# Attention scores of a non-local layer: contraction over 96 rows in one piece, or over three parts of 32 rows on four row groups

## The chip, the cores and the metric

The kernel runs on one core of one Trainium2 chip. The core has five engines, each with its own queue of instructions: TensorE (PE, matrix products; its weight loads are listed separately as PEld), VectorE (DVE), ScalarE (ACT), GpSimd (POOL) and SyncE (SP, which here only issues transfers). The metric is the device time of the whole kernel in microseconds (us); before the change it is 6844.52 us, the median of three runs (6835.98 to 6856.77). All data are 32-bit floats, and every product `nc.tensor.matmul` appears in the trace as two weight loads and two matmuls.

## The reference

A batch of 4 images of 192 channels and 64x64 pixels passes through four layers: a deformable convolution with channel attention and an MLP (layer 0), a non-local block (layer 1), overlapping-window attention with a gated MLP (layer 2), and a per-image depthwise convolution (layer 3). The change concerns layer 1 alone:

```python
g_x     = conv1x1(x, g_w, g_b)          # 96 channels, N = 4096 pixels
theta_x = conv1x1(x, theta_w, theta_b)  # the queries, 96 channels
phi_x   = conv1x1(x, phi_w, phi_b)      # the keys, 96 channels
f1 = einsum('bon,bom->bnm', theta_x, phi_x)   # 4096 x 4096 scores an image
y  = einsum('bnm,bom->bon', softmax(f1, axis=-1), g_x)
return conv1x1(y, W_w, W_b) + x
```

## The kernel before

The images go one after another through the layers. Each image `b` has a **keys stage** (`keys`, from L859), then **layer 1** proper (`layer1`, from L880), then layer 2's windows (L1112 and around it are its scores), and the MLPs with layer 3. Work of the next image is woven in: for images 0, 1 and 2, the gather of the next image's layer 0 (`gather`, L566 to L596, four interpolating operations on ACT and DVE for each of 297 gathers, and products `h`, L590) runs beside layer 1, some 2.5 gathers a step; for images 1 and 2 the offsets of the next image (`offsets`, L431 to L490: layer norm, a table written to DRAM, a convolution `po`) run beside the keys stage. Image 3 has nothing beside it.

**Keys stage.** The image `x` lies in DRAM (`x_drams`), as two halves of 96 channels. For each of 8 chunks of 512 pixels, x is loaded (L865), two products accumulate `phi` (L868) into one bank of PSUM, and ACT copies it with its bias to `ph`, 96 rows by 4096 keys (L869). Eight products make `g` transposed (L873), and DVE copies it to `gx` (L876).

**Layer 1.** The 4096 queries are cut into 16 tiles of 256 (`NQ`, `QN`), the keys into 8 groups of 4 x 128 (`NG`, `G`): 128 steps an image. For each query tile, `load` fetches x (L909), projects it to 96 query channels (L912), and ACT adds the bias (L914). For each step, `score` makes four products of 96 rows, 128 keys, 256 queries (L920) into a PSUM tile `p` of two banks, of which the pool has two; ACT copies it to one of the slots in SBUF (L922), and DVE keeps the running maximum (L925, L927). After a tile's eighth step `negated_max` folds it, transposes it on PE (L936), negates it (L938), spreads it over 128 rows (L941, L944) and copies it (L946).

The scores run ahead of their use: `ahead` is the number of slots, 10 beside a gather and 16 for image 3. The main loop then adds the negated maximum (L983, DVE), takes the exponential (L984, ACT) and multiplies with `gx` into `py` (L986, PE, four products); after each step it issues the scores of the step `ahead` later into the slot just read. `finish` divides by the sum (the gx column of ones), applies `W` (L960), adds the kept x (L961), and stores the result.

**Order.** A planner lays out each engine's queue when the program is built, from the order of the text, estimated durations, and the buffers' becoming free; the hardware runs each queue in that order. `in_turn` pins a constant's load behind what stands before it on SP. PSUM has eight banks: four for the scores, two for `a` and `y`, and two for the gather's `h0`, `h1`.

The central lines of `score`:

```python
for t in range(G):
    nc.tensor.matmul(p[:, t, :], lhsT=ph[:, bass.ts(G * g + t, 128)], rhs=ths[i], start=True, stop=True)
nc.scalar.copy(slot(i, g), p)
```

Of the kernel before, what the change touches and what calls it, by code (L numbers as in the profile page):

```python
# [13 lines left out]
ALU = mybir.AluOpType  # L14
# [33 lines left out]


QN, G, EXTRA = 256, 4, 2  # L50
NQ, NG = HW // QN, HW // 128 // G


# [26 lines left out]
def conv_seq_kernel(ctx: ExitStack, tc: tile.TileContext, a, out: bass.AP):  # L80
    nc = tc.nc

    def pool_of(**kw):

        return tc.tile_pool(**({} if kw.get("space") == DRAM else {"reuse_waits": "tile"}), **kw)
# [78 lines left out]
    for i in range(3):  # L164
# [1 line left out]


    (
        thetaT, phiT, gT, wW, qkvT, bias, v48, headsel, sel6, fc1_dram, fc1_bias, fc1b_dram, fc1b_bias, outb,
    ) = (None for _ in range(14))  # L170

    def in_turn(dma):

# [2 lines left out]
    def late(name, src):  # L176
        t = const(list(src.shape), name)
        in_turn(nc.sync.dma_start(out=t, in_=src))
        return t

    def constants():

        nonlocal thetaT, phiT, gT, wW, qkvT, bias, v48, headsel, sel6, fc1_dram, fc1_bias, fc1b_dram, fc1b_bias, outb
        n128 = sum(m * n for _, m, n in _V128)
        v128 = late("v128", a["v128"])
        at = 0
# [4 lines left out]
        yield  # L191
        thetaT, phiT, gT = (late(n, a[n].rearrange("(k p) n -> p k n", p=P)) for n in ("thetaT", "phiT", "gT"))
        wW = late("wW", a["wW"])

        yield

# [131 lines left out]

    xn_flat = [dram.tile([C, XNW], F32, tag=f"xnd{i}", name=f"xnd{i}") for i in range(2)]
    x_flat = [dram.tile([C, HW], F32, tag=f"xd{i}", name=f"xd{i}") for i in range(2)]  # L330
    xn_drams, x_drams = ([t.rearrange("(k p) n -> p k n", p=P) for t in ts] for ts in (xn_flat, x_flat))

    def variances(pv, sq, mean):
# [525 lines left out]
    def keys(b, ph, gx, sb, ps):  # L859

        nc.gpsimd.memset(gx[:, :, P : P + 1], 1.0)
        for i in range(NCH):
            cols = bass.ts(i, CN)
            x = sb.tile([P, 2, CN], F32, tag="x", name=f"xk_{b}_{i}")
            nc.sync.dma_start(out=x, in_=x_drams[b % 2][:, :, cols])  # L865
            p = ps.tile([128, CN], F32, tag="k", name=f"tp_{b}_{i}")[:P]
            for k in range(2):
                nc.tensor.matmul(p, lhsT=phiT[:, k, :], rhs=x[:, k, :], start=k == 0, stop=k == 1)  # L868
            nc.scalar.activation(ph[:, cols], p, AF.Identity, bias=V["l1_phib"])  # L869
            p = ps.tile([128, CN], F32, tag="k", name=f"g_{b}_{i}")[:, : 4 * P].rearrange("p (j c) -> p j c", j=4)  # L870
            for j in range(4):
                for k in range(2):
                    nc.tensor.matmul(  # L873
                        p[:, j, :], lhsT=x[:, k, bass.ts(j, 128)], rhs=gT[:, k, :], start=k == 0, stop=k == 1
                    )
            nc.vector.tensor_copy(gx[:, bass.ts(i, 4), 0:P], p)  # L876
            yield


    def layer1(b, kv, beside):  # L880

        ph, gx = kv
        with ExitStack() as s:
            keep = s.enter_context(pool_of(name="l1", bufs=1))
            sb = s.enter_context(pool_of(name="l1a", bufs=2))
            ps = s.enter_context(pool_of(name="l1ps", bufs=2, space=PSUM))
            ps1 = s.enter_context(pool_of(name="l1ps1", bufs=1, space=PSUM))
            step = 0
            if beside is not None:
                beside = beside(s)  # L890

# [13 lines left out]

            def load(i):

                x = xs[i] = sb.tile([P, 2, QN], F32, tag="x", name=f"xc_{b}_{i}", bufs=4)
                nc.sync.dma_start(out=x, in_=x_drams[b % 2][:, :, bass.ts(i, QN)])  # L909
                p = ps1.tile([P, QN], F32, tag="a", name=f"th_{b}_{i}")  # L910
                for k in range(2):
                    nc.tensor.matmul(p, lhsT=thetaT[:, k, :], rhs=x[:, k, :], start=k == 0, stop=k == 1)  # L912
                ths[i] = sb.tile([P, QN], F32, tag="th", name=f"ths_{b}_{i}")
                nc.scalar.activation(ths[i], p, AF.Identity, bias=V["l1_thetab"])  # L914

            def score(i, g):

                p = ps.tile([128, G, QN], F32, tag="s", name=f"s_{b}_{i}_{g}")
                for t in range(G):
                    nc.tensor.matmul(p[:, t, :], lhsT=ph[:, bass.ts(G * g + t, 128)], rhs=ths[i], start=True, stop=True)  # L920
                to = slot(i, g)
                nc.scalar.copy(to, p)  # L922
                if g == 1:
                    tops[i] = sb.tile([128, G, QN], F32, tag="top", name=f"top_{b}_{i}")
                    nc.vector.tensor_tensor(tops[i], slot(i, 0), to, ALU.max)  # L925
                elif g > 1:
                    nc.vector.tensor_tensor(tops[i], tops[i], to, ALU.max)  # L927

            def negated_max(i):

# [36 lines left out]
            def next_scores(k):  # L967
                if k < NQ * NG:
                    i, g = divmod(k, NG)
                    if g == 0:  # L970
                        load(i)
                    score(i, g)
                    if g == NG - 1:
                        mbs[i] = negated_max(i)

            for k in range(ahead):
                next_scores(k)
            for k in range(NQ * NG):
                i, g = divmod(k, NG)
                if g == 0:  # L980
                    py = ps1.tile([P + 1, QN], F32, tag="y", name=f"y_{b}_{i}")
                ex = slot(i, g)
                nc.vector.tensor_tensor(ex, ex, mbs[i].unsqueeze(1).to_broadcast([128, G, QN]), ALU.add)  # L983
                nc.scalar.activation(ex, ex, AF.Exp)  # L984
                for t in range(G):
                    nc.tensor.matmul(  # L986
                        py, lhsT=gx[:, G * g + t, :], rhs=ex[:, t, :],
                        start=g == 0 and t == 0, stop=g == NG - 1 and t == G - 1,
                    )
                if g == NG - 1:  # L990
                    y = sb.tile([P + 1, QN], F32, tag="yn", name=f"yn_{b}_{i}")
                    nc.scalar.copy(y, py)  # L992
                    ends.append((k, i, y))
                    if i == NQ - 1:
                        keep_warm(py, 4)
                next_scores(k + ahead)
                if ends and (k >= ends[0][0] + 2 or k == NQ * NG - 1):
                    finish(*ends.pop(0)[1:])
                if beside is not None:
                    beside(k + 1)  # L1000
# [879 lines left out]
    for b in range(B):  # L1880
        with ExitStack() as s:
            sb = s.enter_context(pool_of(name="l1x", bufs=1))
            ph = sb.tile([P, HW], F32, name=f"ph_{b}", tag="ph")
            gx = sb.tile([128, HW // 128, P + 1], F32, name=f"gx_{b}", tag="gx")
            beside, m2, at = None, None, at_second
            if b + 1 < B:
                m2 = stats.tile([M, C + 3 * M], F32, tag="m2", name=f"m2_{b + 1}")
            with ExitStack() as s2:
                making = keys(
                    b, ph, gx, s2.enter_context(pool_of(name="l1k", bufs=2 if 0 < b < B - 1 else 4)),  # L1890
                    s2.enter_context(pool_of(name="l1kps", bufs=2, space=PSUM)),
                )
# [104 lines left out]
```

## Time and profile before

| what | us |
|---|---|
| median of three runs | 6844.52 |
| the profiled execution: its own time, given as its span | 6951.6 |
| PE busy / DVE / ACT / POOL in it | 6255.4 / 4817.8 / 3725.4 / 2061.6 |
| layer 1 of images 0, 1, 2 (909 to 1602, 2516 to 3213, 4135 to 4832) | 693, 697, 697 |
| layer 1 of image 3 (5694 to 6206) | 512 |
| keys stages of images 0 and 3 (856 to 909, 5640 to 5694) | 53, 54 |
| keys stages of images 1 and 2, with offsets (2398 to 2516, 4022 to 4135) | 118, 113 |

The profile is that of one execution, with each instruction's start and length. Engines run at the same time, so their busy times do not add up to the span; what counts in a stage is which engine's wait ends last. A busy PE need not be a PE at its peak, since products are pipelined: a single product of 256 columns is listed with 379 ns, but in a stream the next starts after some 216. So the length of a stream is read from the chain (the work that ended last, followed back from the end), where x8 in 1.73 us means eight instructions. The granted clock is a share of PE's full speed.

### The profile page before, as it was taken

The numbers are of one execution on the slowest core, as the hardware profiler recorded it, in microseconds if no ns is written. First come the engines' busy times: TensorE is split into PE (matmuls) and PEld (weight loads), VectorE is DVE, ScalarE is ACT, GpSimd is POOL, SyncE is SP. The second block draws the span as 40 slices with busy tenths as digits, with TensorE's granted clock in tenths as the row PEclk, the third lists the DMA queues.
The fourth block names the chain that finished last, engine by engine and source line by source line (L and its number), as shares of the span: only waits on it lengthen the run. The fifth ranks groups of instructions, "written<-read, shape, count | busy, mean of one in ns | idle before, by whom it ended". The sixth has DMA issues, their size and how long they took to land.

```text
span 6951.6 us, 115213 instructions
## 1 busy us (share of the span) xinstructions
PE 6255.4 (90%) x45188; PEld 4235.5 (61%) x45188; DVE 4817.8 (69%) x7087; ACT 3725.4 (54%) x6214; POOL 2061.6 (30%) x2273
## 2 busy tenths in 40 slices
PE   7677999999988899999988899999998889999876
PEld 4445578886643468886654458887554457766432
DVE  3664279985577769985586849996576757765656
ACT  3664368874544358874544348885544325545331
POOL 2654057752200047761200017772210000012100
PEclk8888989999999999999989999999998979999988
DMA  7795257751010277762010067673110010010000
GB/s 229 257 317 180 70 161 225 226 180 36 21 28 13 62 237 227 220 214 57 11 42 12 21 216 217 220 222 102 32 29 22 14 52 10 14 36 12 7 3 20
DMA packets 362109, 743.45 MB, mean 107 GB/s; under 512 B 52647, under 2 KB 245335, under 8 KB 360798
## 3 DMA queue, kind: packets, MB, share of 16 engines
q0 software_dynamic: 95616, 469.38, 21.1%
q1 hardware_dynamic: 265950, 266.70, 12.9%
q8 instruction: 356, 5.83, 0.4%
q14 instruction: 187, 1.53, 0.1%
HBM read 628.06 MB, written 106.21 MB: 106 GB/s over the span
## 4 chain that ended last, share of the span: by engine, by line
PE 65%; DVE 17%; ACT 7%; issue 4%; DMA 4%; SPq 1%; another core or an unknown queue 1%; POOL 1%; DVEq 0%; ACTq 0%; POOLq 0%
PE s L920 11%; PE y L986 11%; PE h L590 7%; PE v L1151 2%; DVE ha L1328 2%; PE qk L1076 2%; PE h L1528 2%; DMA ring<-table,idx 2%; PE qk L1077 2%; DVE ga L1328 2%; PE po L482 2%; PE t L1159 1%; PE h L803 1%; DVE gate L1328 1%; PE zm L1539 1%
## 5 line engine op out<-in xcount | busy, mean ns | idle before, releaser
L572 POOL DMA_INDIRECT ring<-table,idx x1188 | 1657.7, 1395 | 1103.3 <-DVE row L579 273.2
L920 PE MATMUL s<-ths,ph 96*128 96x256 f32 x4096 | 981.6, 385 | 14.2 <-ACT ths L914 7.4
L920 PEld LDWEIGHTS s<-ths,ph 96*128 96x128 f32 x4096 | 782.8, 193 | 154.8 <-ACT ths L914 19.0
L578 ACT ACTIVATE row<-ring,pos 128x384 f32<-128x384 f32 x1188 | 697.7, 609 | 213.5 <-DVE xo L583 132.4
L579 DVE SCALAR_TENSOR_TENSOR row<-ring,fr,row 128x384 f32<-128x384 f32 x1188 | 696.9, 611 | 84.1 <-ACT row L578 56.8
L986 PE MATMUL y<-sc,gx 128*97 128x256 f32 x3008 | 720.1, 379 | 0.0
L582 ACT ACTIVATE xo<-row,pos 128x192 f32<-128x192 f32 x1188 | 504.6, 448 | 151.3 <-remote 73.1
L986 PEld LDWEIGHTS y<-sc,gx 128*97 128x97 f32 x3008 | 489.0, 164 | 125.7 <-issue 2.3
L583 DVE SCALAR_TENSOR_TENSOR xo<-row,fr,xo 128x192 f32<-128x192 f32 x1188 | 464.4, 411 | 106.9 <-ACT xo L582 59.6
L590 PE MATMUL h<-ti,xo 128*128 128x192 f32 x2376 | 460.3, 329 | 5.6 <-DVE xo L583 5.6
L922 ACT COPY sc<-s 128x1024 f32<-128x1024 f32 x376 | 377.3, 1003 | 164.1 <-PE s L920 155.1
L983 DVE TENSOR_TENSOR sc<-sc,mbs 128x1024 f32<-128x1024 f32 x376 | 446.7, 1216 | 20.9 <-ACT mbs L946 13.7
L927 DVE TENSOR_TENSOR top<-top,sc 128x1024 f32<-128x1024 f32 x282 | 344.5, 1222 | 149.5 <-ACT sc L922 133.9
L590 PEld LDWEIGHTS h<-ti,xo 128*128 128x128 f32 x2376 | 404.4, 191 | 40.4 <-DVE xo L583 11.7
L984 ACT ACTIVATE sc<-sc 128x1024 f32<-128x1024 f32 x376 | 392.5, 1053 | 39.2 <-DVE sc L983 36.6
L1135 DVE TENSOR_REDUCE es<-ex 128x6 f32<-128x384 f32 x264 | 133.3, 546 | 358.8 <-ACT ex L1131 358.8
L590 PE MATMUL h<-kept,xo 128*128 128x192 f32 x990 | 261.9, 402 | 121.4 <-DVE xo L583 61.7
L1569 POOL COPY gate<-gate 128x192 f32<-128x192 f32 x12 | 4.2, 351 | 1115.2 <-ACT gate L1562 1115.2
L590 PEld LDWEIGHTS h<-kept,xo 128*128 128x128 f32 x990 | 191.2, 226 | 203.6 <-DVE xo L583 92.9
L1328 DVE SCALAR_TENSOR_TENSOR ga<-gate,v,ga 128x1024 f32<-128x1024 f32 x234 | 299.7, 1281 | 7.2
L986 PE MATMUL y<-se,gx 128*97 128x256 f32 x1088 | 260.4, 379 | 0.5 <-ACT yn L992 0.5
L1533 ACT ACTIVATE z<-h,bias_fc1T 128x512 f32<-128x512 f32 x192 | 118.0, 687 | 230.2 <-PE h L1530 229.9
(390 smaller groups left out, 11548.6 us busy)
## 6 DMA issues: line engine op xcount, KB each, us to landing
ti<-table SPq DMA_DIRECT2D x396, 96.0 KB
table<-tt SPq DMA_DIRECT2D x24, 1056.0 KB
ring<-table,idx POOLq DMA_INDIRECT x1188
xnd<-xn SPq DMA_DIRECT2D x4, 3270.0 KB
table<-kept SPq DMA_DIRECT2D x12, 1056.0 KB
table<-tt SPq DMA_DIRECT2D x44, 288.0 KB
xi<-in_x_dram SPq DMA_DIRECT2D x32, 384.0 KB
xk<-xd SPq DMA_DIRECT2D x32, 384.0 KB
```

The source lines that it names most:

```text
L572: nc.gpsimd.indirect_dma_start(out=gt.rearrange("p r q c -> p (r q c)"), out_offset=None, in_=table[:, :], in_offset=bass.IndirectOffsetOn ...
L578: nc.scalar.activation(row, gt[:, :, 0, :], AF.Copy, scale=pos[:, t, 9 + tap : 10 + tap])
L579: nc.vector.scalar_tensor_tensor(row, gt[:, :, 1, :], fr[:, t, 9 + tap : 10 + tap], row, ALU.mult, ALU.add)
L582: nc.scalar.activation(xo[:, j, :], row[:, 0, :], AF.Copy, scale=pos[:, t, tap : tap + 1])
L583: nc.vector.scalar_tensor_tensor(xo[:, j, :], row[:, 1, :], fr[:, t, tap : tap + 1], xo[:, j, :], ALU.mult, ALU.add)
L590: nc.tensor.matmul(acc[m // 2][:, bass.ts(m % 2, C)], lhsT=xo.rearrange("p j c -> p (j c)")[:, bass.ts(m, 128)], rhs=tt, start=t == 0 and ...
L920: nc.tensor.matmul(p[:, t, :], lhsT=ph[:, bass.ts(G * g + t, 128)], rhs=ths[i], start=True, stop=True)
L922: nc.scalar.copy(to, p)
L983: nc.vector.tensor_tensor(ex, ex, mbs[i].unsqueeze(1).to_broadcast([128, G, QN]), ALU.add)
L984: nc.scalar.activation(ex, ex, AF.Exp)
L986: nc.tensor.matmul(py, lhsT=gx[:, G * g + t, :], rhs=ex[:, t, :], start=g == 0 and t == 0, stop=g == NG - 1 and t == G - 1,)
L1328: nc.vector.scalar_tensor_tensor(acc[:, b], src(tap, b), w[:, tap : tap + 1], acc[:, b], ALU.mult, ALU.add)
```

## The change

Keys and queries are kept as 3 parts (`KP`) of 32 channels, and the 128 rows of SBUF hold four groups (`RG`) of 32 rows. In the keys' tile `ph`, now 128 rows by 3 by 1024, row group r holds key tile r of each chunk. In the queries' tile every row group holds the same queries.

A score step takes four key tiles, one a row group, three products each, accumulated; two steps go in one burst into one PSUM tile of four banks, a bank for each row group, of which the pool now has one. Two copies and up to two maxima follow. The burst comes after every second step of the main loop.

Keys and queries are both projected in the keys stage by `rows_of`: 24 products of 96 rows by 32 columns each a chunk, on four column groups of the output. DVE adds the biases (from `rowb`, loaded by eight small transfers among the constants). The queries are written to DRAM (`th_dram`) and come back in `load` as four transfers a tile, one a row group, issued half a tile ahead. ACT copies `gx` in DVE's place. The image tile `x`, still wanted by `finish`, is loaded by `load_given` at a tile's first step, with three buffers in place of four.

```diff
+RG, KP = 4, 3
+KN = HW // RG
...
+        rowb = const([128, 2, KP], "rowb")
+        for r in range(RG):
+            to = rowb[32 * r : 32 * r + 32]
+            for n, col in enumerate((n96 - 1, n96 - 2)):
+                in_turn(nc.sync.dma_start(out=to[:, n, :], in_=a["v96"][:, col : col + 1].rearrange("(j c) n -> c (j n)", c=32)))
...
+    th_dram = dram.tile([NCH, 128, KP * 128], F32, tag="thd", name="thd")
...
+        def rows_of(w, x, name):
+
+            p = ps.tile([128, CN], F32, tag="k", name=name)[:, : KP * 128].rearrange("p (j n) -> p j n", j=KP)
+            for j in range(KP):
+                for k in range(2):
+                    for r in range(RG):
+                        nc.tensor.matmul(
+                            p[32 * r : 32 * r + 32, j, :], lhsT=w[:, k, 32 * j : 32 * j + 32], rhs=x[:, k, bass.ts(r, 128)],
+                            start=k == 0, stop=k == 1,
+                        )
+            return p
+
+        def plus(to, p, n):
+            nc.vector.tensor_tensor(to, p, rowb[:, n, :].unsqueeze(2).to_broadcast([128, KP, 128]), ALU.add)
...
-            p = ps.tile([128, CN], F32, tag="k", name=f"tp_{b}_{i}")[:P]
-            for k in range(2):
-                nc.tensor.matmul(p, lhsT=phiT[:, k, :], rhs=x[:, k, :], start=k == 0, stop=k == 1)
-            nc.scalar.activation(ph[:, cols], p, AF.Identity, bias=V["l1_phib"])
+            plus(ph[:, :, bass.ts(i, 128)], rows_of(phiT, x, f"tp_{b}_{i}"), 0)
+            th = sb.tile([128, KP, 128], F32, tag="th", name=f"thk_{b}_{i}", bufs=2)
+            plus(th, rows_of(thetaT, x, f"tt_{b}_{i}"), 1)
+            nc.sync.dma_start(out=th_dram[i], in_=th.rearrange("p j n -> p (j n)"))
...
-            nc.vector.tensor_copy(gx[:, bass.ts(i, 4), 0:P], p)
+            nc.scalar.copy(gx[:, bass.ts(i, 4), 0:P], p)
...
-            ps = s.enter_context(pool_of(name="l1ps", bufs=2, space=PSUM))
+            ps = s.enter_context(pool_of(name="l1ps", bufs=1, space=PSUM))
...
-                x = xs[i] = sb.tile([P, 2, QN], F32, tag="x", name=f"xc_{b}_{i}", bufs=4)
+                t = sb.tile([128, 2, KP, 128], F32, tag="th", name=f"ths_{b}_{i}")
+                of = th_dram[i // 2].rearrange("(t c) n -> c t n", c=32)[:, bass.ts(i % 2, 2)]
+                for r in range(RG):
+                    nc.sync.dma_start(out=t[32 * r : 32 * r + 32].rearrange("p t j n -> p t (j n)"), in_=of)
+                ths[i] = t
+
+            def load_given(i):
+                x = xs[i] = sb.tile([P, 2, QN], F32, tag="x", name=f"xc_{b}_{i}", bufs=3)
                 nc.sync.dma_start(out=x, in_=x_drams[b % 2][:, :, bass.ts(i, QN)])
-                p = ps1.tile([P, QN], F32, tag="a", name=f"th_{b}_{i}")
-                for k in range(2):
-                    nc.tensor.matmul(p, lhsT=thetaT[:, k, :], rhs=x[:, k, :], start=k == 0, stop=k == 1)
-                ths[i] = sb.tile([P, QN], F32, tag="th", name=f"ths_{b}_{i}")
-                nc.scalar.activation(ths[i], p, AF.Identity, bias=V["l1_thetab"])
...
-                p = ps.tile([128, G, QN], F32, tag="s", name=f"s_{b}_{i}_{g}")
-                for t in range(G):
-                    nc.tensor.matmul(p[:, t, :], lhsT=ph[:, bass.ts(G * g + t, 128)], rhs=ths[i], start=True, stop=True)
-                to = slot(i, g)
-                nc.scalar.copy(to, p)
...
+                p = ps.tile([128, RG, 2, QN], F32, tag="s", name=f"s_{b}_{i}_{g}")
+                for u in range(2):
+                    for j in range(KP):
+                        for r in range(RG):
+                            rows = slice(32 * r, 32 * r + 32)
+                            nc.tensor.matmul(
+                                p[:, r, u, :].rearrange("p (t n) -> p t n", t=2), lhsT=ph[rows, j, bass.ts(g + u, 128)],
+                                rhs=ths[i][rows, :, j, :], start=j == 0, stop=j == KP - 1,
+                            )
+                for u in range(2):
+                    to = slot(i, g + u)
+                    nc.scalar.copy(to, p[:, :, u, :])
...
-                    if g == 0:
-                        load(i)
+                    if k == 0:
+                        load(0)
+                    if g == NG // 2 and i + 1 < NQ:
+                        load(i + 1)
                     score(i, g)
-                    if g == NG - 1:
+                    if g == NG - 2:
                         mbs[i] = negated_max(i)
...
-            for k in range(ahead):
+            for k in range(0, ahead, 2):
                 next_scores(k)
             for k in range(NQ * NG):
                 i, g = divmod(k, NG)
                 if g == 0:
+                    load_given(i)
...
-                next_scores(k + ahead)
+                if k % 2:
+                    next_scores(k - 1 + ahead)
...
-            ph = sb.tile([P, HW], F32, name=f"ph_{b}", tag="ph")
+            ph = sb.tile([128, KP, KN], F32, name=f"ph_{b}", tag="ph")
```

More of the change, by code (lines that the diff above doesn't have):

```diff
@@ L168, in conv_seq_kernel @@
     (
-        thetaT, phiT, gT, wW, qkvT, bias, v48, headsel, sel6, fc1_dram, fc1_bias, fc1b_dram, fc1b_bias, outb,
-    ) = (None for _ in range(14))
+        thetaT, phiT, gT, wW, qkvT, bias, v48, headsel, sel6, fc1_dram, fc1_bias, fc1b_dram, fc1b_bias, outb, rowb,
+    ) = (None for _ in range(15))
     def in_turn(dma):
@@ L183, in constants @@
         nonlocal thetaT, phiT, gT, wW, qkvT, bias, v48, headsel, sel6, fc1_dram, fc1_bias, fc1b_dram, fc1b_bias, outb
+        nonlocal rowb
         n128 = sum(m * n for _, m, n in _V128)
@@ L885, in layer1 @@
             sb = s.enter_context(pool_of(name="l1a", bufs=2))
-            ps = s.enter_context(pool_of(name="l1ps", bufs=2, space=PSUM))
+            ps = s.enter_context(pool_of(name="l1ps", bufs=1, space=PSUM))
             ps1 = s.enter_context(pool_of(name="l1ps1", bufs=1, space=PSUM))
-            step = 0
             if beside is not None:
@@ L916, in score @@
-            def score(i, g):
-                p = ps.tile([128, G, QN], F32, tag="s", name=f"s_{b}_{i}_{g}")
-                for t in range(G):
-                    nc.tensor.matmul(p[:, t, :], lhsT=ph[:, bass.ts(G * g + t, 128)], rhs=ths[i], start=True, stop=True)
-                to = slot(i, g)
-                nc.scalar.copy(to, p)
[L923 to L927, printed above, removed]
+                t = sb.tile([128, 2, KP, 128], F32, tag="th", name=f"ths_{b}_{i}")
@@ new lines, in load @@
+                of = th_dram[i // 2].rearrange("(t c) n -> c t n", c=32)[:, bass.ts(i % 2, 2)]
[4 more added lines that the diff above has]
+                x = xs[i] = sb.tile([P, 2, QN], F32, tag="x", name=f"xc_{b}_{i}", bufs=3)
+                nc.sync.dma_start(out=x, in_=x_drams[b % 2][:, :, bass.ts(i, QN)])
+            def score(i, g):
+                p = ps.tile([128, RG, 2, QN], F32, tag="s", name=f"s_{b}_{i}_{g}")
[10 more added lines that the diff above has]
+                    nc.scalar.copy(to, p[:, :, u, :])
+                    if g + u == 1:
+                        tops[i] = sb.tile([128, G, QN], F32, tag="top", name=f"top_{b}_{i}")
+                        nc.vector.tensor_tensor(tops[i], slot(i, 0), to, ALU.max)
+                    elif g + u > 1:
+                        nc.vector.tensor_tensor(tops[i], tops[i], to, ALU.max)
```

## The prediction

> **What bounds the kernel now.** I read the page first: its busy line, the chain that ended last, and the two costliest matmul groups.
>
> ```profile
> PE 6255.4 (90%) x45188; PEld 4235.5 (61%) x45188; DVE 4817.8 (69%) x7087; ACT 3725.4 (54%) x6214; POOL 2061.6 (30%) x2273
> PE s L920 11%; PE y L986 11%; PE h L590 7%; PE v L1151 2%; DVE ha L1328 2%; PE qk L1076 2%; PE h L1528 2%; DMA ring<-table,idx 2%; PE qk L1077 2%; DVE ga L1328 2%; PE po L482 2%; PE t L1159 1%; PE h L803 1%; DVE gate L1328 1%; PE zm L1539 1%
> L920 PE MATMUL s<-ths,ph 96*128 96x256 f32 x4096 | 981.6, 385 | 14.2 <-ACT ths L914 7.4
> ```
>
> TensorE (PE) leads, and the scores (L920) are the first entry of the chain. The 4096 records are 2048 products: every fp32 product runs as two instructions. PE waited only 14.2 us ahead of them. Next I cut the span into stages; the columns are the stretch, its length, then busy us (and instruction count) of PE, PE weight loads, VectorE (DVE), ScalarE (ACT) and POOL, granted clock, DMA share and GB/s.
>
> ```profile
> core 0: us, PE busy (x) PEld busy (x) DVE busy (x) ACT busy (x) POOL busy (x), PEclk, DMA share, GB/s
> 1300.00:1425.00 125.00, 124.42 (x619) 104.57 (x618) 119.69 (x196) 105.97 (x183) 92.65 (x64) 1.00 0.75 234
> 2620.00:2870.00 250.00, 244.28 (x1196) 204.42 (x1196) 231.40 (x375) 205.46 (x351) 185.69 (x119) 0.99 0.70 218
> 4200.00:4400.00 200.00, 199.33 (x986) 167.55 (x987) 190.35 (x311) 170.24 (x289) 155.32 (x95) 1.00 0.71 221
> 1425.00:1602.00 177.00, 173.06 (x891) 145.02 (x890) 136.88 (x220) 116.03 (x193) 68.62 (x52) 1.00 0.44 137
> 5640.00:5694.00 54.00, 52.44 (x167) 35.07 (x165) 4.46 (x8) 5.46 (x8) 0.00 (x0) 0.56 0.26 68
> 5694.00:6206.00 512.00, 502.63 (x2295) 396.94 (x2295) 356.00 (x381) 268.43 (x305) 1.30 (x2) 0.98 0.04 13
> ```
>
> The first three rows are the steady part of layer 1 for images 0, 1 and 2, with the next image's gather woven in. They hold 896 score instructions, thus 112 steps of 8: a query tile of 8 steps takes 41.1 us. PE is busy 98.8% (40.6 us of a tile), DVE 94.2% (38.7 us), ACT 83.8% (34.4 us). So PE bounds it, but DVE stands 5% behind. The fourth row is the last part of such an image, where the gather thins out: DVE only 77%. The last row is image 3 without a gather: DVE 70%, PE alone in front. The row above it is image 3's keys stage, nearly all PE, at 0.56 of the clock.
>
> From the chain in order of time (start, us, what), in and before layer 1:
>
> ```profile
> 1118.44 1.73 PE y L986 x8
> 1120.16 1.73 PE s L920 x8
> 1176.80 0.87 PE th L912 x4
> 2472.58 2.72 PE po L482 x32
> 2475.30 0.44 PE pv_l L339 x16
> 882.24 3.41 PE tp L868 x4
> 885.65 3.36 PE g L873 x16
> ```
>
> A score step costs PE 1.73 us, 216 ns an instruction, 0.845 ns a column; the query projection 0.87 us a tile. L482 and L339 are products of 96 rows by 32 columns on four column groups of the array: 85 ns for 384 columns and 27.5 ns for 128, where one at a time would be 324 and 108 ns. They run 3.8 to 3.9 at once.
>
> **The scores.** 96 rows become 3 parts of 32, so 12 products (24 instructions) a step in place of 4 (8), four at once if row groups overlap. No row has four row groups of 128 columns. The nearest is the window scores, three row groups of 32x64 (timeline: start, us, engine, line, shapes, count):
>
> ```profile
> 1628.76 0.78 PEld L1112 LDWEIGHTS s<-ks,qw 32*64 32x64 f32 x48
> 1628.76 0.92 PE L1112 MATMUL s<-ks,qw 32*64 32x64 f32 x48
> 4103.65 11.17 PE L482 MATMUL po<-xn,wp 96*32 96x384 f32 x134
> ```
>
> The last of the 48 takes 217 ns by itself, so the pace is (920-217)/47 = 15 ns, where 64 columns alone would be 54: 3.6 at once, though its column half changes only every twelfth instruction. Row groups do overlap in fp32. I take 3.9, as in L482 and L339: 216/3.9 = 55.4 ns, a burst of two steps 48 x 55.4 = 2.66 us, and 0.11 for entering and leaving (8 of L482 take 0.78 us, not 0.67): 2.77 against 3.46. **0.69 us saved a burst**, 256 bursts.
>
> Two rules of the Trainium skill speak against this. "TensorE: Matmul & The Clock Gate", Part 3 (Packing small matmuls), gives 3.07 times, not 4, for four row tiles with K=32. With it a burst is 48 x 216/3.07 = 3.38 + 0.11 us: nothing saved. But the page's own span model is one product's latency plus some ns per tile, so a ratio of single packs, fill included; ours is a stream, and the streamed rows above show 3.6 to 3.9. The same page, LDWEIGHTS, makes a load's time follow its columns, 128/1.2 = 107 ns (an estimate from the page), whatever its rows. Loaded one after another, 48 take 5.1 us, 1.8 more than now per burst. The row decides: 64 columns would be 53 ns by the rule, and L1112's 48 loads came 14 ns apart. Loads of different row groups overlap, and 107 ns fits beneath its own group's 216.
>
> **The single score buffer.** Two tiles of two banks become one of four, so each burst waits for both copies (L922, 1.0 us each) of the one before. In image 3 PE has y (2 x 1.73) and other work (about 0.6), 4.1 us, against 2 copies, perhaps one exp (1.05) ahead of them and 0.2 of hand-over, 3.3 us: hidden. With gather the cover is 6.5 us or more, but ACT is 84% busy. Behind a waiting burst in PE's queue stand y, the gather's products h, and the maxima's transposes; ACT and DVE wait for those. I take nothing in steady state (0 to 1 us a burst). In the fill, with no y to cover it, bursts and copies alternate: image 3's first 8 steps took 17.5 us and become 4 x (2.7 to 5.5, by the clock, +2.1), 19 to 30; with the other 8 steps +8 us. The other images' fill (10 steps in 29 us) is held by ACT and DVE already: +2 each.
>
> **The maximum's chain.** Steps 6 and 7 now come together, so the negated maximum comes a copy and a max later, 1 to 2 us; next late is the first addition (L983) of the next tile, its exp and its y. PE's cover there is two y, h and a burst, about 8.6 us, against a chain of 9: up to 1 us a tile. DVE has gather work meanwhile. This is in the utilization taken next.
>
> **Layer 1 with gather.** PE per tile: 40.6 - 4 x 0.69 - 0.87 = 37.0 us. DVE keeps 38.7 and becomes the bound. If it ran as full as PE does now (98.8%), a tile would take 39.2; at the 94.2% of today, 41.1. I take 97%, 39.9, as two engines must now both run near full: 1.2 saved, times 11.9 tiles (938 to 1425 us) = 14. The last part is PE's: 24 score steps, 12 x 0.69, and three projections of 0.87 = 11. Less 2 for the fill: 23 an image, **-69** for three. **Image 3:** 56 bursts x 0.69 + 16 x 0.87 - 8 = **-44**.
>
> **The keys stage.** A chunk's keys were 4 instructions, 1.72 us at full clock (3.41 at half). Keys and queries are now 48 each of L339's very shape: 48 x 27.5 = 1.32 us each, 2.64. That is 0.92 more a chunk, 7.4 us for each of images 1 and 2; images 0 and 3 run this stage mostly at half clock, 1.87 a chunk, about 13 each. **+41**. Should packed products let the clock rise, these two stages would be some 15 us shorter than now, the lower bound. DVE takes two additions for one copy (0.56 us), ACT a copy for an activation (0.68): both nearly idle in image 3, 40% busy in images 1 and 2. Eight writes of 196 KB an image queue on SP; behind one that waits for its addition stand the next chunk's loads (L865) and the layer norm's (L431). They fall in the first half of the stage, where the DMA share is 0.3 to 0.4.
>
> **Loads.** Each tile issues four query loads on SP (0.31 us each by L865's median, 1.2 us of 41) and still loads x, later. They are issued four steps (20 us) ahead, and behind them stand the gather's ti loads. 0.39 MB a tile is 9.6 GB/s beside 220: hidden, and if the cover is gone, a late tile costs the landing, some us. POOL gains no instruction. At the four stage starts and for eight small bias loads I put **+3**. ACT loses 0.47 us a tile, uncounted.
>
> **Sum:** -69 - 44 + 41 + 3 = -69 us. The profiled execution spans 6951.6 us, 107 more than the median 6844.5 of the timed runs; the stages are the same work, so I carry the difference over whole: **6775 us**.
>
> **Rivals.**
> (1) DVE gives no more than now: only the ends of the three images gain, 3 x 9, and image 3's 44: 6845 - 27 - 44 + 44 = 6818. For it: DVE's 96% in the first row; against: PE reaches 99.5% in that same row.
> (2) Slower: a burst waits for ACT's copies of the burst before. In the 92 bursts of image 3 and the image ends each us of it counts whole; in the other 141, beyond the 0.72 us that DVE's bound forgives. A mean wait of 0.75 us eats the gain; 1 us gives 92 + 39 = 131, so 6906. For it: ACT's 84% and its strict order behind gather work; against: PE's longest wait for a score copy today is 1.5 us.
> (3) The change doesn't do what it says: row groups give 3.07, about 6845; or loads come one by one, 64 x 1.79 - 14 = 101 an image and the keys' 41, about 7290. L1112 speaks against both.
> (4) DVE reaches 98.8% and the keys' clock rises: about 6700.
>
> **How the numbers follow.** Mine 0.50 (6740 to 6815), (1) 0.16, (2) 0.21, (3) 0.05 and 0.02, (4) 0.06. Faster by over 0.3% (20 us; the three runs lie 0.3% apart): mine, (4) and over half of (1), 0.65. Within: the rest of (1), most of the first of (3) and waits near 0.75 us, 0.13. Slower: most of (2) and the rest, 0.22. The range 6700 to 6915 leaves out the second of (3), (2) with longer waits, and half of (4).
>
> **What would show it.** The score group at 12288 records and some 55 ns apart; PE's tile at 37 us, DVE at 96% or more in the three steady stretches, a tile of 40 us; image 3's layer 1 near 468 us. Wrong if score bursts wait for score copies by over 0.7 us on average, if their loads come over 55 ns apart, or if PE's clock falls in layer 1.

## The result and the profile after

The change makes the kernel slower: 7303.24 us, median of four runs (7290.89 to 7318.74), against 6840.25 us (6816.69 to 6856.77, four runs) before. The ratio is 1.0688, with an interval of 1.0659 to 1.0717. I had forecast 6775. The profile of the kernel before is of an execution of 6951.6 us, 111 above its median, so sums of stages taken against it are rough.

From the page of the changed kernel: the busy line, the chain's shares by engine, the group of the scores, and that of the output projection.

```profile
PE 6244.1 (85%) x56068; PEld 4168.3 (57%) x56068; DVE 4873.9 (67%) x7119; ACT 3712.0 (51%) x6150; POOL 1870.1 (26%) x2273
PE 48%; DVE 25%; ACT 11%; issue 6%; DMA 6%; SPq 2%; POOL 1%; DVEq 0%; ACTq 0%; POOLq 0%
L950 PE MATMUL s<-ths,ph 32*128 32x256 f32 x12288 | 851.6, 413 | 168.0 <-ACT sc L956 118.5
L994 PE MATMUL wy<-yn,wW 96*96 96x256 f32 x256 | 99.1, 475 | 172.6 <-DVE yn L989 170.3
```

No engine became the bound: all four are less busy, as shares, than before. PE fell from 90% to 85% and leads only 48% of the chain (65% before). It now sits idle for 168 us ahead of the scores (14.2 before), most of it until ACT has copied a score tile, and for 173 us ahead of the small product `wy`, of which there are only two a query tile.

The same by stages, with the columns of the table shown for before; the first two rows are steady parts of layer 1 with a gather beside, the third is image 3.

```profile
1200.00:1400.00 200.00, 175.35 (x1430) 141.60 (x1422) 168.34 (x271) 145.93 (x250) 117.55 (x87) 0.94 0.68 209
2800.00:3050.00 250.00, 216.56 (x1734) 173.91 (x1733) 213.11 (x344) 181.04 (x309) 143.64 (x105) 0.95 0.67 206
6100.00:6400.00 300.00, 250.19 (x2144) 181.46 (x2144) 181.20 (x193) 132.14 (x145) 0.00 (x0) 0.91 0.08 22
```

PE is busy 88%, 87% and 83% of the time, DVE 84%, 85% and 60%, and the granted clock fell from 1.00 (0.98 in image 3) to between 0.91 and 0.95. Taking a query tile from one copy of its maximum (L980) to the next, over 11 tiles from the second on, the period went from 42.2 to 47.5 us in images 0 to 2, and from 31.0 to 36.8 us in image 3. From first score to last `y`, layer 1 is longer by 84, 99, 96 and 96 us in the four images. That is 375 of the 463 us between the medians; 65 more are in the four keys stages, measured against the old ones where they run at full clock (in the run of the bursts alone, below).

The packed products themselves did what they were meant to. From the timeline of PE (start, us, engine, line, shapes, count), one burst:

```profile
6145.48 2.87 PE L950 MATMUL s<-ths,ph 32*128 32x256 f32 x48
```

In the trace the four instructions of the four row groups start within 20 ns, and the next four 216 ns after them: 54 ns an instruction, 4.0 times the pace of one at a time. Their weight loads start in the same fours. A wrong multiple is not the cause. What stands before such a burst is. The chain of the changed kernel in image 3, in order of time:

```profile
6130.67 0.38 ACT mbs L980
6131.05 0.02 issue
6131.08 9.17 DVE sc L1020 x8
6140.25 0.34 DVE yn L989
6140.59 0.04 issue
6140.63 1.17 PE wy L994 x2
6141.80 3.32 PE y L1023 x8
```

and PE's timeline at the same place (in brackets the idle time before, and what ended it):

```profile
6132.83 0.59 PE L988 MATMUL pd<-rd,ones 1*96 1x256 f32 x2
6133.36 1.97 PE L1023 MATMUL y<-se,gx 128*97 128x256 f32 x8
6140.63 1.17 PE L994 MATMUL wy<-yn,wW 96*96 96x256 f32 x2 [5.30 <-DVE yn L989]
6141.59 3.53 PE L1023 MATMUL y<-se,gx 128*97 128x256 f32 x8
```

`wy` projects the tile just finished and needs `yn`, which DVE makes from `pd`. PE had made `pd` by 6133.4. But DVE's queue holds the eight additions of the next tile ahead of `yn`, 9.17 us of them, and PE's queue holds `wy` ahead of products that were ready (`y`, then a burst). So PE stands still for 5.30 us. Then it runs at half clock, here in the columns of the stages above:

```profile
6141.00:6145.00 4.00, 4.00 (x11) 2.65 (x11) 1.53 (x2) 1.79 (x2) 0.00 (x0) 0.51 0.00 0
```

In the chain `wy` takes 1.17 us, not 0.43, and the next eight `y` 3.32, not 1.73: 2.3 us on top of the wait. Before, PE's queue held a score step between the two, in the chain of that kernel:

```profile
6060.61 0.60 PE pd L954 x2
6061.21 1.92 PE s L920 x8
6063.14 0.43 PE wy L960 x2
```

The list of PE's waits in image 3 of the changed kernel (microseconds in all, times, the longest) says that it is so in nearly every tile, 12 times in 500 us, and that nothing else there comes near it:

```profile
PE wy L994 <- DVE yn L989: 61.9, 12, 5.3
PE mt L970 <- DVE top L967: 10.8, 13, 1.6
```

Beside a gather a second wait comes to it. Over the whole kernel the scores wait for ACT's copies of an earlier score tile, in the slots of `sc` and of `se`:

```profile
PE s L950 <- ACT sc L956: 118.5, 42, 4.4
PE s L950 <- ACT se L956: 20.9, 8, 4.4
```

Before, such waits were 2.7 us in all. Both waits point to the order of the queues, and the next section puts that to the test.

### The profile page after: what moved, and what is told of

Same layout as the page of the kernel before. It is cut to its first block, busy times and chain, and to the rows that moved or that the text cites. A ratio compares the mean times of both kernels' runs of the same rounds, so it can differ in the third digit from the quotient of the medians.

```text
span 7306.3 us, 137675 instructions
## 1 busy us (share of the span) xinstructions
PE 6244.1 (85%) x56068; PEld 4168.3 (57%) x56068; DVE 4873.9 (67%) x7119; ACT 3712.0 (51%) x6150; POOL 1870.1 (26%) x2273
## 4 chain that ended last, share of the span: by engine, by line
PE 48%; DVE 25%; ACT 11%; issue 6%; DMA 6%; SPq 2%; POOL 1%; DVEq 0%; ACTq 0%; POOLq 0%
PE y L1023 7%; PE s L950 5%; PE h L600 4%; DMA ring<-table,idx 4%; DVE sc L1020 3%; DVE row L589 2%; PE v L1189 2%; DVE ha L1366 2%; PE qk L1114 2%; DVE ga L1366 2%; PE h L1566 2%; DVE se L1020 2%; PE qk L1115 2%; ACT row L588 2%; PE po L492 1%
## 5 line engine op out<-in xcount | busy, mean ns | idle before, releaser
L582 POOL DMA_INDIRECT ring<-table,idx x1188 | 1468.0, 1236 | 1555.7 <-DVE row L589 632.9
L950 PE MATMUL s<-ths,ph 32*128 32x256 f32 x12288 | 851.6, 413 | 168.0 <-ACT sc L956 118.5
L950 PEld LDWEIGHTS s<-ths,ph 32*128 32x128 f32 x12288 | 668.9, 201 | 314.8 <-ACT sc L956 137.6
L1023 PE MATMUL y<-sc,gx 128*97 128x256 f32 x3008 | 744.9, 393 | 1.3 <-ACT sc L1021 1.2
L1023 PEld LDWEIGHTS y<-sc,gx 128*97 128x97 f32 x3008 | 507.6, 171 | 154.2 <-issue 17.5
L956 ACT COPY sc<-s 128x1024 f32<-128x1024 f32 x376 | 360.4, 1010 | 302.1 <-PE s L950 283.8
L1020 DVE TENSOR_TENSOR sc<-sc,mbs 128x1024 f32<-128x1024 f32 x376 | 440.2, 1221 | 14.2 <-ACT mbs L980 13.0
L1023 PE MATMUL y<-se,gx 128*97 128x256 f32 x1088 | 277.2, 402 | 2.9 <-ACT se L1021 2.3
L994 PE MATMUL wy<-yn,wW 96*96 96x256 f32 x256 | 99.1, 475 | 172.6 <-DVE yn L989 170.3
```

The source lines that it names most:

```text
L582: nc.gpsimd.indirect_dma_start(out=gt.rearrange("p r q c -> p (r q c)"), out_offset=None, in_=table[:, :], in_offset=bass.IndirectOffsetOn ...
L950: nc.tensor.matmul(p[:, r, u, :].rearrange("p (t n) -> p t n", t=2), lhsT=ph[rows, j, bass.ts(g + u, 128)], rhs=ths[i][rows, :, j, :], sta ...
L956: nc.scalar.copy(to, p[:, :, u, :])
L1023: nc.tensor.matmul(py, lhsT=gx[:, G * g + t, :], rhs=ex[:, t, :], start=g == 0 and t == 0, stop=g == NG - 1 and t == G - 1,)
```

## The experiments

The planner of this kernel lays out the queues from estimated durations, and I take it to add the estimates of products one after another. Before, two score steps are 8 products of 256 columns, now they are 24. They run four at once, but the plan would then count a burst as three times as long as the two steps it replaces. Theory A says that this wrong price gave a bad order, and that the order costs the 7%. Theory B says that the change's own parts cost it: the burst of two steps in a single score buffer, which holds a burst until ACT has copied the one before (rival 2 of the prediction). Later runs take up my rival 1, that DVE is the bound once PE is relieved.

For A the kernel is traced twice while it is built. The first program is only planned, with the prices altered; the second is the whole kernel, and each engine is pinned to the order of the first.

**Bursts alone.** The kernel before, with two steps in a burst into one four-bank buffer; operands and products unchanged:

```diff
-            ps = s.enter_context(pool_of(name="l1ps", bufs=2, space=PSUM))
+            ps = s.enter_context(pool_of(name="l1ps", bufs=1, space=PSUM))
...
-                p = ps.tile([128, G, QN], F32, tag="s", name=f"s_{b}_{i}_{g}")
+                p = ps.tile([128, G, 2, QN], F32, tag="s", name=f"s_{b}_{i}_{g}")
+                for u in range(2):
...
-                next_scores(k + ahead)
+                if k % 2:
+                    next_scores(k - 1 + ahead)
```

> The kernel before with only its score steps put together two and two: one PSUM tile of four banks, one buffer, products of 96 rows, no row groups, queries projected as before. Theory A (the queues' order: the planner lays out all engines' queues as if each row-group product ran alone, so the packed burst ends long before its planned time and ACT, DVE and PE stand in an order made for slow scores): this kernel has no row groups, so it stays near the kernel before, 6840 to 6920 us. Theory B (the single four-bank buffer and the burst: each burst waits for both copies, and the run-ahead is a step shorter): most of the loss is here, 7100 to 7250 us. Theory C (the packed products themselves: switching of the array, weight loads, the clock): as before, 6840 us.

6892.17 us, ratio 1.0091 (1.0059 to 1.0124). Of the 57 us, image 3 has 38 by its profile (layer 1 takes 549 us, 511 before): its tiles take 32.6 us and not 31.0. With a gather beside there is no loss in the period (41.8). So theory B is real in image 3, 0.6 us for each of its 64 bursts, and the run as a whole loses an eighth of the result. It has an order of its own, too, so how much of this is the buffer stays open.

**The change's instructions in an order planned at the right price.** In the plan only a quarter of the packed products is counted, those of row group 0 in `score` and of column group 0 in `rows_of`:

```diff
+                            if plan and r:
+                                continue
-                            nc.tensor.matmul(
+                            mm = nc.tensor.matmul(
...
+                            if r:
+                                extras.add(mm.ins.name)
...
+    nc = build(False, build(True))
```

> The changed kernel, instruction for instruction, but with the order of every queue taken from a plan in which only one of four packed products (scores and projections) is counted, so that the planner's price of a burst is near what it takes. Theory A: the loss goes, and the freed PE shows: 6740 to 6850 us, layer 1 of image 3 under 490 us. Theory B and C: the single buffer or the packed products hold it up in any order, 7150 to 7320 us.

6833.51 us, ratio 0.9994 (0.9972 to 1.0016). The whole loss is gone, with the same instructions. A tile takes 41.5 us beside a gather and 28.2 in image 3. There the wait of 5.3 us and the 2.3 us of half clock make 7.6 of the 8.6 us by which the changed kernel's tile is longer.

**The kernel before in an order planned at the wrong price.** Its instructions are untouched; in the plan each score product is counted three times:

```diff
-                    nc.tensor.matmul(p[:, t, :], lhsT=ph[:, bass.ts(G * g + t, 128)], rhs=ths[i], start=True, stop=True)
+                    for again in range(3 if plan else 1):
+                        mm = nc.tensor.matmul(
+                            p[:, t, :], lhsT=ph[:, bass.ts(G * g + t, 128)], rhs=ths[i], start=True, stop=True
+                        )
```

> The kernel before, instruction for instruction, but with the order of every queue taken from a plan in which each score product is counted three times. Theory A: the wrong order alone costs most of what the change cost, 7100 to 7300 us. Theories B and C: nothing in this kernel is packed or shares a buffer, so it stays at 6840 us, give or take 50.

7326.65 us, ratio 1.0715 (1.0679 to 1.0751): the loss of the change, without the change. From the waits of this kernel between 2700 and 3250 us, and of the changed one in the same stretch:

```profile
PE wy L965 <- DVE yn L960: 33.2, 11, 5.2
```

```profile
PE wy L994 <- DVE yn L989: 26.7, 10, 4.8
```

The wait before `wy` appears in both, so it needs no row groups. So does the wait for score copies; over the whole kernel, first with the old instructions in the wrong order and then with the change in good order:

```profile
PE s L921 <- ACT sc L927: 103.5, 60, 6.1
```

```profile
PE s L956 <- ACT sc L964: 35.4, 34, 2.0
```

The first kernel has two score buffers and waits more, the second has one and waits less, so it is the order that makes most of this wait, and not the buffer. The waits don't stand in the same places: in image 3 the old instructions in the wrong order wait for score copies (39.8 us in 500), where the changed kernel waits for `yn`. Pinning by itself is no cure, since both runs are pinned. That the order costs the 7% is shown in both directions; the factor of three in the price is my count of products, not a measurement.

**Which queue carries it.** The good order on ACT and DVE only; PE and the transfers are laid out at the wrong price:

```diff
-                if "Manual" in type(i).__name__:
+                if "Manual" in type(i).__name__ or str(i.engine).split(".")[-1] not in ['Activation', 'DVE', 'ACT']:
```

> The changed kernel, with the order of the good plan (one of four packed products counted) for the queues of ACT and DVE alone; PE, SP and POOL are ordered by the planner with its own price. Theory A in its narrow form (ACT and DVE hold work ahead of the copies and of what PE waits for; PE's own order does little harm): most of the loss goes, 6830 to 6950 us. In its wide form (every queue must fit the others): half or more of the loss stays, above 7000 us.

7464.14 us, ratio 1.0712 (1.0687 to 1.0737). This run and those of `halfmax96`, `halfmax_replanned` and `hybrid` were on a chip where the kernel before takes 6973 us; ratios hold within a chip. Image 3 recovers (31.3 us a tile), but the images with a gather get worse, 52.6 us a tile. From the waits of 500 us in image 1, for this kernel and then for the one in good order throughout:

```profile
ACT sc L964 <- PE s L956: 72.2, 23, 6.5
```

```profile
ACT sc L964 <- PE s L956: 14.2, 23, 1.3
```

ACT's queue now asks for bursts that PE's queue has placed later. A good order on these two queues is not enough; they have to fit PE's. A good order on PE alone was not tried.

**Is DVE the bound?** First the kernel before, and then the change in good order, with the maximum taken over every second key group. The softmax is the same with any shift near the maximum, so nothing of the outputs is left out; DVE has four maxima of 1.22 us less a tile.

```diff
-                if g == 1:
+                if g == 2:
...
-                elif g > 1:
+                elif g in (4, 6):
```

> The kernel before with the running maximum taken over key groups 0, 2, 4 and 6 alone: three maxima on DVE a tile in place of seven, 4.9 us less DVE work a tile; the softmax is the same for any shift. Theory D1 (PE bounds the kernel before, in all images): next to nothing, 6780 to 6840 us. Theory D2 (DVE already limits the images with a gather): a tile there gets 2 to 4 us shorter, 6680 to 6760 us.

6914.22 us, ratio 0.9911 (0.9888 to 0.9934), at the edge of what D1 forecast. A tile beside a gather takes 41.6 us and not 42.2, where D2 had 2 to 4 us less.

> The changed kernel in the order of the good plan, with maxima over groups 0, 2, 4 and 6 alone (4.9 us less DVE work a tile). Theory D1 (with the score products packed, PE needs 37 to 38 us a tile and DVE's 39 is what held a tile at 41.5 in the images with a gather): a tile there goes to 38 to 39.5 us and the kernel to 6700 to 6760 us, more than the same edit brings the kernel before. Theory D2: the gain is that of the kernel before, no more.

7091.17 us, ratio 1.0174 (1.0148 to 1.0201), the opposite of what either theory had. Its tiles with a gather take 46.5 us. This kernel had a plan of its own, made without the four maxima. So it was repeated in the order of the good run, planned with the maxima in it (`halfmax_pinned` below): the same instructions then take 0.9974, on another chip. The 2% was again the order: a right price does not make sure of a good one.

**What holds the good order at 1.00.** PE's timeline of the run in good order shows bursts cut by the gather's products `h` into pieces, mostly of 8 to 40 instructions. Counting from the start of each piece to the start of the next, less idle time, and scaling to a tile (192 score instructions, 64 before) gives this, over 400 us of steady work in each of images 0 to 2:

| per tile, us | before | good order | bursts whole | changed kernel |
|---|---|---|---|---|
| scores | 14.1 | 12.4 | 11.2 | 12.8 |
| pieces they come in | 8 | 10 | 4 | 5 |
| PE idle | 0.7 | 1.0 | 3.6 | 6.4 |

Four whole bursts would be 4 x 2.77 = 11.1 us by the prediction. Theory P: the cuts make PE the bound. Theory D: DVE is. In `glued` a burst's 48 instructions are kept together in PE's order, at the place of the first:

```diff
+        whole = {}
+        for n in places:
+            whole.setdefault(bursts.get(groups[n][0].name, n), []).append(n)
+        places = [n for w in whole.values() for n in w]
```

> The same kernel as the run named replanned, for the three that follow to stand beside. If the order of the queues is all that the change got wrong, its ratio to the kernel before is again 0.997 to 1.002 on whatever chip; if its 0.9994 was a matter of that chip, it is above 1.01, as the run with half of the maxima and a plan of its own was.

6827.35 us, ratio 0.9999 (0.9978 to 1.0020), on a third chip.

> The run named replanned, with every burst of 48 instructions kept whole in TensorE's queue: the plan had put convolution products into it and so cut many bursts into pieces of 8 to 32. In the stretch from 1200 to 1400 us of replanned, 19.3 bursts took 64.8 us of TensorE where 19.3 x 2.80 would be 54, so the cuts cost some 0.55 us a burst, 2.2 us a tile; TensorE was 97% busy there (40.2 us a tile of 41.5) and VectorE 94% (39.2). Theory P, the cuts make TensorE the bound of the gather images: 38.0 us of TensorE a tile, the period falls to 40.4, where VectorE is at 97%, 48 tiles x 1.1 = 53 us, ratio 0.990 to 0.995. Theory D, VectorE is the bound already: within 15 us of replanned, ratio 0.997 to 1.002.

6901.90 us, ratio 1.0102 (1.0064 to 1.0140).

> The run named replanned in its order, without four of a tile's maxima over key groups (the maximum over half of the groups serves the softmax as well, the outputs agree): 4 x 1.22 = 4.9 us of VectorE less a tile. The order of all other instructions is the one planned with these maxima in it. Theory D (VectorE is the bound): the period falls from 41.5 to TensorE's 40.2 and a little, 48 tiles x 0.5 to 1.2 = 25 to 60 us, ratio 0.991 to 0.996. Theory P (TensorE is, through the cut bursts): within 20 us of replanned. A ratio over 1.01 would say that the slow run with half of the maxima was not slow by its order.

6816.99 us, ratio 0.9974 (0.9959 to 0.9988).

> Both edits, whole bursts and half of the maxima (the outputs agree). Both theories: TensorE 38.0 us a tile, VectorE 34.3, the period 38.5 to 39.5 in the images with a gather, 48 tiles x 2.0 to 3.0 = 96 to 144 us below replanned, ratio 0.979 to 0.986; image 3 unchanged. If it is no lower than the better of the two edits alone, a third thing bounds these images (the gather's chain of ring, ACT and DVE, or the order of the queues itself).

6873.62 us, ratio 1.0057 (1.0036 to 1.0078). The stretch from 1200 to 1400 us of the good order, then of its form with half of the maxima, then with whole bursts:

```profile
1200.00:1400.00 200.00, 193.99 (x1578) 144.86 (x1578) 188.71 (x310) 164.04 (x281) 155.92 (x99) 1.00 0.75 234
```

```profile
1200.00:1400.00 200.00, 192.94 (x1577) 146.87 (x1576) 170.06 (x292) 164.70 (x285) 137.37 (x99) 1.00 0.77 239
```

```profile
1200.00:1400.00 200.00, 182.68 (x1510) 143.43 (x1512) 179.96 (x294) 157.37 (x270) 153.26 (x90) 0.98 0.71 220
```

And with both edits at once:

```profile
1200.00:1400.00 200.00, 183.44 (x1550) 146.38 (x1549) 164.38 (x284) 159.74 (x280) 139.55 (x98) 0.99 0.75 234
```

With DVE at 85% in place of 94%, PE stays 96% busy and the tile period moves from 41.5 to 41.3. Theory D falls. But P's remedy failed too. Whole bursts bring the scores down to 11.2 us a tile, as computed, and PE then waits 2.6 us more a tile, for `h` operands and exponentials that come at the pace of the old order. With both edits PE is 92% busy and DVE 82%, and the kernel is still slower than in good order with neither. So a third thing holds these images, as the last expectation had it for this case: not the work of one of the two engines alone, but the order of the queues or the chain of the gather. Which of the two, these runs do not separate. What the cuts cost PE, they cover elsewhere. Whether a plan that knows of whole bursts would do better is open; I only moved instructions within one plan.

**A version that beats both.** Images 0 to 2 as before the change, image 3 packed, all planned at the right price:

```diff
+            plain = b < B - 1
...
-            layer1(b, (ph, gx), beside)
+            (layer1_96 if plain else layer1)(b, (ph, gx), beside)
```

> Images 0, 1 and 2 keep the keys stage and layer 1 of the kernel before; image 3, which has no gather, has the packed scores; all in an order planned with one of four packed products counted. Theory A with D1: image 3's tile was 31.2 us and becomes 28.8, its layer 1 some 30 us shorter and its keys stage some 8 longer: 6800 to 6825 us, faster than both kernels. If packing brings nothing even where PE alone is in front: 6835 to 6860 us.

6942.88 us on the slower chip, ratio 0.9952 (0.9933 to 0.9971), inside what theory A had. Then with half of the maxima in images 0 to 2:

> The run named hybrid, and in images 0 to 2 the maxima over half of the key groups, as in the run named halfmax96 (the outputs agree). If the two gains stand beside each other, 0.9952 x 0.9911 = 0.986 of the kernel before, 0.983 to 0.990; they belong to different images, so only the planned order ties them together. If the order of the queues comes out differently because a tile has four instructions less, as it did in halfmax_replanned, the ratio is anywhere from 0.99 to 1.02.

6795.27 us, ratio 0.9946 (0.9922 to 0.9970), 43 us below the 6838.25 of the kernel before beside it. By ratio this is no better than `halfmax96` alone (0.9911) or `hybrid` alone: the two gains do not multiply. Layer 1's tiles are where both put them (41.6 and 28.2 us); from these 48 x 0.6 + 16 x 2.8 = 74 us should come, less some 9 for image 3's longer keys. Why `halfmax96` gained some 60 us on the slower chip when its tiles gain 29 is not traced.

## Why the prediction was wrong

**The step that failed** is the one from PE's work to the tile's time: "PE per tile: 40.6 - 4 x 0.69 - 0.87 = 37.0 us", taken at 97% of whichever engine is fullest. It assumes that PE finds ready work as before. My description of the kernel said that a planner lays out each queue from estimated durations, and the forecast did not ask what the planner would make of 24 products where 8 stood. By my count it made a burst of 10 us (three times 3.46, an estimate) of one of 2.8. `wy` stood in PE's queue long before `yn` was due in DVE's, bursts stood ahead of copies that came late, and PE idles some 6 us a tile, where beside a gather it had idled 0.7. None of my rivals named the order. Rival 2 named one of the two waits: bursts waited for score copies, 0.54 us each on average (139.4 us over 256), below the 0.75 that it needed to eat the gain. The single buffer, its reason, is not what made most of them. Of my three signs of being wrong one came, the fall of the clock, to between 0.90 and 0.94 over layer 1. The second case of rival 3 lands on 7290 by chance: the loads that it lets come one by one came four at a time.

**The sum in good order.** The run in good order tests the other terms. Layer 1 and keys stages are compared by their lengths in the profiles, keys against those of the burst run, whose keys stages are the old ones at full clock (30, 110, 114, 31 us; now 46, 125, 124, 39).

| term | predicted | measured in good order |
|---|---|---|
| layer 1, images 0 to 2 | -69 | -12, -11, -14 = -37 |
| layer 1, image 3 | -44 | -34 |
| keys stages | +41 | +16, +14, +10, +9 = +49 |
| loads | +3 | not seen apart |
| sum | -69 | -22; medians -2 and -8 |

The 14 to 20 us between that sum and the medians are not placed. Had the old keys stages of images 0 and 3 run at half clock in the timed executions, as in the profile of the kernel before (49 and 54 us), it would be some 42 us more. So even with the queues right the change is worth nothing that shows.

**A burst** saves 0.49 us, not 0.69. In the chain of image 3 in good order:

```profile
5809.30 3.63 PE y L1031 x16
5812.93 2.80 PE s L956 x48
5815.73 3.62 PE y L1031 x16
5819.36 2.80 PE s L956 x48
```

Two steps take 6.43 us where they took 6.92. The pace, 54 ns, is better than the 55.4 I took, and the two rules that the prediction weighed, 3.07 times and one load after another, were rightly set aside for this stream. But twelve fours of 216 ns are 2.59 us and sixteen `y` 3.46, so changing over costs 0.21 us in the burst and 0.17 in the `y` after it, some 0.4 and not 0.11. In the images with a gather the planner cuts the bursts, 10 pieces a tile, and pays a price at each cut; `h` also goes from 169 to 183 ns an instruction, counted like the table of pieces. Of the 2.8 us a tile that I gave to packing, 1.7 came.

**DVE as the next bound** (my "39.9 us a tile" and rival 1): in good order a tile gains 0.7 us (42.2 to 41.5), where I had 1.2 and rival 1 nothing. The sizes are near, but by luck: `halfmax_pinned` takes DVE down to 85% and gains 0.2 us more.

**The single buffer**, taken at nothing in image 3: bursts of the old products into it cost 38 us there, in that run's own order. With the change in good order it costs nothing in image 3: the chain above alternates 16 `y` and a burst without a gap, and two copies (1.0 us each) fit beneath 3.6 us of `y`.

**The keys** were costed too low for images 1 and 2 (7.4 us each, measured 14 and 10). For images 0 and 3 I had 13 each at half clock. Against old stages at full clock they lost 16 and 9, image 0 at a mean clock of 0.93. But image 3's packed stage ran at full clock throughout, so against the old one of the profile, 54 us at half clock, it is 15 us shorter: the rise of the clock that my lower bound allowed for.

## What to carry to other kernels

When products are packed on row or column groups and queues are laid out from estimates, ask first what price the layout puts on them: here it was some three times too high, and cost 7%. Look for it where a small product waits long for an engine whose queue holds later work ahead of its operand. To separate order from work, run the new instructions in an order planned at the right price, and the old instructions in one planned at the wrong price. Don't take a right price for a good order either: with less work and the right price, one plan here was 2% slower. And count packed bursts as whole in the estimate of gain only where the plan leaves them whole; each change between packed and whole-array products has its price.

## What the runs showed of the hardware

In image 3 of the changed kernel, twelve waits of 5.3 us before `wy` each went with 6.83 us at half clock, which began some 2.5 us before the wait ended. Each such wait cost some 2.3 us more than it lasted (`wy` and eight `y` in 4.49 us, not 2.16). The mean clock of layer 1 was 0.90 to 0.94, and 0.98 to 0.99 with the same instructions in good order.

Fp32 row groups of 32 rows by 128 columns run at 54 ns an instruction for 256 columns, four at once, and changing between them and whole-array products costs about 0.4 us there and back (6.43 us for 16 `y` and a burst, where 28 times 216 ns would be 6.05).

The keys stage of image 3 is nearly all PE (52.4 of 54 us before). With the old products it took 53.9 to 54.5 us at a mean clock of 0.55 to 0.56 in three profiled executions (`before`, `misplanned`, `halfmax96`) and 30.7 at full clock in a fourth (`burst96`); with the packed ones it took 39.2 to 40.0 us at full clock in all ten. In image 0 both kinds vary: 29.5 to 51.9 us with the old products. Why is not traced.
